# Query weights scaled later, shared down tiles moved behind the experts, and a norm begun one layer earlier, in a two-layer transformer kernel

## The chip, the cores and the metric

The kernel runs on one core of one Trainium2 chip. A core has five engines with queues of their own: TensorE (PE, with weight loads PEld beside it), VectorE (DVE), ScalarE (ACT), GpSimd (POOL) and SyncE (SP, which here issues most DMAs). Each engine takes its instructions in order and waits at the front of its queue for semaphores of the others. The metric is device microseconds (us) of one execution.

## The reference, cut to what matters

Two transformer layers work on the residual stream x of 4 sequences of 512 tokens, 256 wide. Each has an attention and an FFN half, each with a layer norm, a shift and scale, and a gate g from a conditioning vector c:

```python
h = layernorm(x) * (1 + ca) + sa;   x = x + ga * attention(h)
h = layernorm(x) * (1 + cb) + sb;   x = x + gb * ffn(h)
```

Layer 0's attention is linear (normalised q times a sum of normalised k times v). Its FFN is a mixture of 32 experts, 6 to a token:

```python
buf = zeros((E * C + 1, h)).at[slot].set(x[tok_idx])        # C = 48 places per expert
gu = einsum('ech,ehf->ecf', xb, w_gate_up); g, u = split(gu, 2)
yb = einsum('eci,eih->ech', silu(g) * u, w_down)
out = einsum('tk,tkh->th', topk_w, yflat[slot])
out = out + (silu(x @ ws_gate) * (x @ ws_up)) @ ws_down     # the shared expert
```

Layer 1's attention has 16 heads of 128 with a causal mask over T = 512 tokens of a sequence:

```python
logits = einsum('bthd,bThd->bhtT', q, k) * rsqrt(128);  out = softmax(logits + mask) @ v @ w_o
```

Its FFN is gated, with weights made from control points by a spline.

## The kernel before

**Order.** The order of PE is the order in which the code issues its matmuls; for the stretch around the change it is written out by hand (the block `tc.manual_schedule`, L953). The other engines' instructions are ordered by a scheduler by priority and readiness in its own model, except that `tc.issue_after(x)` puts what it encloses behind x on x's engine. An instruction without such a tie can be put far ahead of its place in the code. Buffers come from pools: a tile with `tag` and `bufs=n` is a ring of n, and a new tile waits until all work on the one n before it is done.

**Layer 0's end.** After the linear attention the 32 experts are done in 16 pairs, q = 0 to 15. `fetched(q)` (L793) gathers a pair's token rows, with their weights and target places, from a table in DRAM into a tile `xg` by an indirect DMA of POOL. `turned(q)` (L802) transposes them on PE, and DVE copies them to `xT`. `gate_up(q)` (L809) multiplies by the pair's weights; ACT makes silu, DVE the product `act`. `act_turned(q)` (L825) transposes that. `down(q)` (L832) makes `y`, which ACT weighs into `ysb` (a ring of four; pairs 12 to 15 have another four). Three things then leave `ysb`: an indirect DMA of POOL scatters it into the array `planes` in DRAM (pairs 0 to 11 only), a DMA of SP writes it to the table `ytab`, and, for pairs 12 to 15, `combined(q)` (L890) adds it on PE by a one-hot matrix. Expert weights `wg` and `wd` are in rings of eight, loaded on SP as slots come free.

The loop of L960 to L989 runs for each q, on PE: gate_up(q+1), act_turned(q), turned(q+2), one shared down in the first iterations, down(q-1), combined(q-2). `shared_down(i)` (L724) is the down product of the shared expert for token tile i of 16: three matmuls into a PSUM bank `pd`, and a copy to `ysum` by ACT. Before, tiles 0 to 3 stand ahead of the loop, 4 to 9 in its iterations 0 to 5, 10 and 11 around the last `combined`, and 12 to 15 at the end of the block. Only sequence 0 is combined here, to let layer 1 begin: `read_back` (L917) loads its sums from `planes` into `yr` once all scatters have landed, `gated` (L932) adds them to x on POOL and DVE, and `add_transposed` adds what pairs 12 to 15 gave. The other sequences are gathered from `ytab` later, under layer 1.

**Into layer 1.** `scale_q(n)` (L767) multiplies the query weights of head n by a constant, on ACT; the first three are issued at L1010, behind the block, with no tie. `norm(0)` (L1167, called at L1495) norms sequence 0: statistics on DVE, a power on POOL (L196, `last_pow`), the normed `xn` half on DVE and half on ACT, transposes on PE into `lt_a`, and `hT_a` from these by ACT and DVE. `hT` tiles are in a pool `hp1` (L1021). POOL then makes the first weight forms (`weight_forms`, L1183 to L1191, sums of blocks of weights, since products here use seven block products for eight).

**Layer 1's head loop** (L1519 to L1589) runs n = 0 to 64 over 4 x 16 heads. Among the work of a head are the next head's projections (`project`), scores, softmax and values of this and the one before, on POOL the weight forms of a later head, and one unit of the spline for the FFN weights in every second head. At units 1, 4 and 7, that is at heads 8, 14 and 20, four POOL subtractions `ffn_forms` (L1061) follow. Heads 11, 27 and 43 issue the next sequence's `norm`; heads around multiples of 16 issue gathers of `ytab`. Head 59 issues the norm of the FFN of sequence 0, `ffn_norm(0)` (L1082, L1586), untied.

## Time and profile before

| | |
|---|---|
| median of 3 executions | 1165.59 us (1163.98 to 1167.76) |
| profiled execution | 1165.69 us |
| its span | 1164.0 us, and 1.69 us around it |
| mean granted PE clock | 0.992 |
| busy, share of the span | PE 96%, PEld 71%, DVE 73%, POOL 53%, ACT 47% |
| DMA | 86.09 MB, mean 74 GB/s |

The experts lie between about 150 and 225 us, the passage into layer 1 up to about 245 us, the head loop up to the spline FFN at the end. A line of the timeline gives start, duration, engine, code line, operation, output and inputs, and in brackets how long the engine had been idle before it and what ended that. A line of the waits gives in total, how often and the longest wait of an engine at one place. PE can be granted half its clock after idle time, and the windows of the profile list what it was granted (1.00 is the full clock).

### The profile page before, as it was taken

How to read it: one execution, taken by the hardware profiler on the slowest of the kernel's cores; microseconds unless marked ns; L12 is line 12 of the kernel's file. 1: busy time of each engine (PE TensorE's matmuls, PEld its weight loads, DVE VectorE, ACT ScalarE, POOL GpSimd, SP SyncE). 2: the span in 40 equal slices, each digit the busy share in tenths (PEclk: the TensorE clock that was granted, in tenths of full speed). 3: DMA queues.
4: the chain of work that ended last, by engine and by line, in shares of the span. 5: the costliest groups of instructions: out<-in, count | busy, mean ns of one | idle time of the engine just before them, and what ended most of it. 6: DMA issues, size and time to landing. Idle time of an engine off the chain costs nothing.

```text
span 1164.0 us, 16910 instructions
## 1 busy us (share of the span) xinstructions
PE 1118.4 (96%) x5231; PEld 822.6 (71%) x5231; DVE 850.9 (73%) x2573; ACT 541.5 (47%) x1380; POOL 621.0 (53%) x944
## 2 busy tenths in 40 slices
PE   7888999989999999999999999999999999999998
PEld 2444364557777777777777777777787777888887
DVE  5687534567878887888887887988877777566765
ACT  3652223345555555555555465555555455333321
POOL 4363224248874857864656975444635655344331
PEclk9998999899999999999999999999999999999999
DMA  7921379734411322520321431012010000000001
GB/s 264 289 68 46 98 238 287 223 101 95 77 46 53 67 68 38 91 68 28 78 40 43 95 64 60 28 37 69 19 46 19 25 13 1 1 1 19 19 1 36
DMA packets 80485, 86.09 MB, mean 74 GB/s; under 512 B 12158, under 2 KB 64748, under 8 KB 80268
## 3 DMA queue, kind: packets, MB, share of 16 engines
q1 hardware_dynamic: 67868, 70.19, 19.3%
q0 software_dynamic: 11712, 13.25, 7.2%
q10 hardware_dynamic: 816, 1.58, 0.4%
q8 instruction: 42, 0.69, 0.2%
q14 instruction: 47, 0.39, 0.1%
HBM read 73.84 MB, written 11.55 MB: 73 GB/s over the span
## 4 chain that ended last, share of the span: by engine, by line
PE 72%; DVE 8%; POOL 4%; ACT 3%; issue 2%; DMA 2%; SPq 0%; ACTq 0%; POOLq 0%; DVEq 0%
PE s L1308 10%; PE o L1349 10%; PE po L1044 7%; PE P0p L1044 6%; PE fP L1044 6%; PE pt L1340 5%; PE P1p L1044 4%; PE P2p L1044 4%; PE acc L1044 3%; PE P0v L1044 3%; PE P2v L1044 2%; PE P1v L1044 2%; POOL ysum L281 1%; PE gu L814 1%; PE sg L713 1%
## 5 line engine op out<-in xcount | busy, mean ns | idle before, releaser
L1323 ACT ACTIVATE p<-s,nm 128x512 f32<-128x512 f32 (+3 forms) x256 | 135.4, 529 | 117.2 <-DVE nm L1320 114.7
L1308 PE MATMUL s<-qk,qk 128*128 128x512 f32 (+3 forms) x512 | 170.1, 434 | 1.1 <-DVE qk L1216 1.0
L1349 PE MATMUL o<-pT,v 128*128 128x512 f32 (+3 forms) x512 | 148.8, 433 | 0.3 <-DVE u3v L1228 0.3
L1349 PEld LDWEIGHTS o<-pT,v 128*128 128x128 f32 x512 | 96.8, 190 | 55.4 <-issue 30.6
L1342 ACT COPY pT<-pt 128x512 f32<-128x512 f32 (+1 forms) x192 | 98.5, 513 | 68.2 <-PE pt L1340 66.5
L1320 DVE TENSOR_REDUCE nm<-s 128x1 f32<-128x512 f32 (+3 forms) x256 | 124.0, 484 | 4.0
L281 POOL DMA_INDIRECT ysum<-ytab,code x72 | 113.6, 1578 | 20.4 <-issue 15.2
L1325 DVE TENSOR_SCALAR p<-p,den 128x512 f32<-128x512 f32 (+3 forms) x256 | 116.9, 457 | 3.4
L1340 PEld LDWEIGHTS pt<-ident,p 128*128 128x128 f32 x640 | 81.6, 141 | 34.5 <-issue 10.5
L1340 PE MATMUL pt<-ident,p 128*128 128x128 f32 x640 | 101.7, 273 | 0.3 <-DVE p L1325 0.3
L1318 DVE TENSOR_TENSOR s<-s,mask 128x128 f32<-128x128 f32 x256 | 73.5, 287 | 32.3 <-PE s L1308 32.3
L1183 POOL TENSOR_TENSOR w_p<-w_q,w_k 128x128 f32<-128x128 f32 x63 | 38.9, 617 | 84.3 <-ACT t1p L1222 51.9
L1308 PEld LDWEIGHTS s<-qk,qk 128*128 128x128 f32 x512 | 77.5, 191 | 5.5 <-issue 1.1
L1044 PE MATMUL P0p<-hT_a,w_q 128*128 128x256 f32 x252 | 75.0, 379 | 0.0
L1191 POOL TENSOR_TENSOR w_p<-w_k 128x128 f32<-128x128 f32 x63 | 29.9, 475 | 81.3 <-PE P2p L1044 81.3
L1044 PEld LDWEIGHTS P0p<-hT_a,w_q 128*128 128x128 f32 x252 | 47.5, 190 | 33.1 <-issue 29.9
L1324 DVE RECIPROCAL den<-den 128x1 f32<-128x1 f32 x256 | 40.4, 158 | 38.5 <-ACT p L1323 34.4
L1044 PE MATMUL P1p<-fT,w_p 128*128 128x256 f32 x252 | 65.0, 380 | 2.4 <-POOL w_p L1185 1.3
L1360 ACT ACTIVATE oH<-o,bia 128x512 f32<-128x512 f32 x64 | 44.0, 687 | 42.7 <-PE o L1349 41.5
L1216 DVE SCALAR_TENSOR_TENSOR qk<-P0p,bia,u3p 128x256 f32<-128x256 f32 x63 | 30.4, 482 | 37.4 <-ACT qk L1237 36.2
L1052 POOL TENSOR_TENSOR fI<-it 128x256 f32<-128x256 f32 x30 | 21.8, 728 | 67.0 <-DVE it L1641 67.0
L1044 PEld LDWEIGHTS P1p<-fT,w_p 128*128 128x128 f32 x252 | 47.6, 190 | 10.1 <-issue 2.2
(336 smaller groups left out, 2676.9 us busy)
## 6 DMA issues: line engine op xcount, KB each, us to landing
wg<-in_w_gate_up SPq DMA_DIRECT2D x16, 704.0 KB
w_q<-in_w_q SPq DMA_DIRECT2D x64, 128.0 KB
w_k<-in_w_k SPq DMA_DIRECT2D x64, 128.0 KB
w_v<-in_w_v SPq DMA_DIRECT2D x16, 512.0 KB
wd<-in_w_down SPq DMA_DIRECT2D x16, 352.0 KB
basis<-in_basis SPq DMA_DIRECT2D x8, 640.0 KB
planes<-zero SPq DMA_DIRECT2D x4, 768.0 KB
yr<-planes SPq DMA_DIRECT2D x4, 768.0 KB
```

The lines of the kernel that those rows point to most:

```text
L281: ga = nc.gpsimd.indirect_dma_start(out=ysum[b][:, i, :], out_offset=None, in_=ytab[:, :], in_offset=bass.IndirectOffsetOnAxis(ap=code[:, ...
L1044: nc.tensor.matmul(out, lhsT=lhsT, rhs=rhs, start=start, stop=stop, skip_group_check=shared)
L1308: nc.tensor.matmul(s[:, at[i] : c], lhsT=qk[n, 0][:, i * P : (i + 1) * P], rhs=qk[n, 1][:, : (i + 1) * P], start=True, stop=True,)
L1318: nc.vector.tensor_tensor(s[:, e - P : e], s[:, e - P : e], mask, ALU.add)
L1320: nc.vector.tensor_reduce(nm, s[:, e - w : e], AX.X, ALU.max, negate=True)
L1323: nc.scalar.activation(p, s[:, e - w : e], AF.Exp, bias=nm, accum_out=den)
L1324: nc.vector.reciprocal(den, den)
L1325: nc.vector.tensor_scalar_mul(p, p, den)
L1340: nc.tensor.transpose(pt[:, c : c + P], probs[n, i][:, j * P : (j + 1) * P], ident)
L1342: nc.scalar.copy(pT, pt[:, :w])
L1349: nc.tensor.matmul(o[:, j * P :], lhsT=vs[n // 4][:, j, hc : hc + HD], rhs=pTs[n, j], start=(j == 0), stop=(j == NTT - 1),)
L1360: nc.scalar.activation(oT, o, AF.Identity, bias=bia[:, 2, h : h + 1])
```

## The change

1. `scale_q(0)` to `scale_q(2)` are tied on ACT behind the copy of shared down tile 9, which now stands in the tail.
2. Three shared down tiles leave the loop (iterations 3 to 5). The tail has tiles 7 and 8 around the last `combined`, 9 to 14 behind it, and 15 behind the transposes of the norm. Tiles from 9 on alternate over two banks, `su0` and `su1`, by the new `NTAIL`.
3. The ring of `xg` has seven tiles for eight, and seven gathers are issued ahead for eight.
4. Layer 1's first norm is issued inside the block of layer 0: `xn` in a freed slot of the expert weights (class `Freed`), `lt_a` in the PSUM ring `gu`, `hT` in the pool `w4` with a ring of two; the pool `hp1` goes. ACT's half of `xn` is tied behind the copy of tile 13, and tile 15 stands behind the transposes on PE.
5. `ffn_forms` of units 0, 1 and 2 are issued at heads 8, 15 and 24, tied behind the last weight form.
6. `ffn_norm(0)` at head 59 is tied behind that head's eviction.

The number of instructions is the same on every engine.

```diff
+NTAIL = 7
@@ new_hT
-        return pool.tile([P, 2, T], F32, tag="hT", name=f"hT_{name}{b}")
+        return pool.tile([P, 2, T], F32, tag="hT", name=f"hT_{name}{b}", bufs=B if name[1] == "0" else 2)
@@ layer 0
+        class Freed:
+            def __init__(self, tag, pair):
+                self.tag, self.pair = tag, pair
+            def tile(self, shape, dtype, tag, name, bufs=None):
+                return freed(self.tag, self.pair, shape, name)
...
-            pd = psa.tile([P, D], F32, tag=f"su{i % 2 if i < NEXP or i >= NI - 4 else 0}", name=f"pd{i}", bufs=1)
+            pd = psa.tile([P, D], F32, tag=f"su{i % 2 if i < NEXP or i >= NI - NTAIL else 0}", name=f"pd{i}", bufs=1)
...
-                xg[q] = xp.tile([P, ROW], F32, tag="xg", name=f"xg{q}", bufs=8)
+                xg[q] = xp.tile([P, ROW], F32, tag="xg", name=f"xg{q}", bufs=7)
...
-                if q + 8 < NPAIR:
-                    fetched(q + 8)
-            for q in range(8):
+                if q + 7 < NPAIR:
+                    fetched(q + 7)
+            for q in range(7):
                 fetched(q)
...
-                    if q < NI - NEXP - 6:
+                    if q < NI - NEXP - NTAIL - 2:
                         shared_down(NEXP + q)
...
-                shared_down(NI - 6)
+                shared_down(NI - NTAIL - 2)
                 combined(NPAIR - 1)
-                shared_down(NI - 5)
+                shared_down(NI - NTAIL - 1)
...
-                for i in range(NI - 4, NI):
-                    last_down = shared_down(i)
+                for i in range(NI - NTAIL, NI - 1):
+                    pd_copy = shared_down(i)
+                    if i == NI - NTAIL:
+                        with tc.issue_after(pd_copy.ins):
+                            for n in range(3):
+                                scale_q(n)
+                    if i == NI - 3:
+                        before_norm = pd_copy
+                hTs1[0] = new_hT(w4, 0, "a1")
+                ln_transposed(
+                    Freed("wg", NPAIR - NLOAD + NTT), ps, "gu", 1, 0, SA, CA, hTs1[0], "a1", None, None, before_norm
+                )
+                with tc.issue_after(last_pow[0].ins):
+                    shared_down(NI - 1)
...
-        for n in range(3):
-            scale_q(n)
...
-    hp = ctx.enter_context(tc.tile_pool(name="hp1", bufs=2))
@@ head loop
-        norm(0)
+        EARLY_FORMS = (8, 15, 24)
...
-                if unit in (1, 4, 7):
-                    ffn_forms(unit // 3, early[:, unit // 3])
...
+            if n in EARLY_FORMS:
+                with tc.issue_after(last_form[0].ins):
+                    ffn_forms(EARLY_FORMS.index(n), early[:, EARLY_FORMS.index(n)])
...
-                ffn_norm(0)
+                ffn_norm(0, evicted[n])
```

## The prediction

> **What bounds the kernel.** I read the page's busy shares first, then TensorE's (PE's) waits, then the instructions around the long ones, then what the DMA engines did there. On the page:

> ```profile
> PE 1118.4 (96%) x5231; PEld 822.6 (71%) x5231; DVE 850.9 (73%) x2573; ACT 541.5 (47%) x1380; POOL 621.0 (53%) x944
> ```

> PE is busy for all but 46 us of the 1164.0 us span. The instruction counts of the changed kernel are the same on every engine, so it can only win PE's idle time, and matmul time spent at a lowered clock. PE's waits that the change touches:

> ```profile
> PE gu L814 <- DVE xT L807: 4.1, 1, 4.1
> PE lt_a L226 <- ACT xn_a L208: 3.0, 1, 3.0
> PE P2v L1044 <- DVE v L1215: 2.3, 3, 1.9
> PE P1p L1044 <- POOL w_p L1185: 1.3, 1, 1.3
> ```

> Columns: total us, times, longest. The first two stand between the experts and layer 1, the others inside the head loop. In the order of time the first looks like this (start, us, engine; in brackets the idle time and what ended it):

> ```profile
> 204.85 0.42 ACT L770 ACTIVATE w_q<-w_q 128x256 f32<-128x256 f32 x1 [5.22 <-DMA w_q<-in_w_q]
> 206.37 2.61 PE L814 MATMUL gu<-wg,xT 128*64 128x352 f32 x8 [4.07 <-DVE xT L807]
> 209.93 1.66 PE L837 MATMUL y<-wd,actT 88*64 88x256 f32 x8
> ```

> ACT stands still 5.22 us in a scaling that waits for its weights. Behind it on ACT are the activations of the expert pairs; DVE's xT stands behind their products, and PE runs dry. The stage table shows what follows (columns: PE, PEld, DVE, ACT, POOL busy, granted PE clock, DMA share, GB/s):

> ```profile
> 200.00:205.00 5.00, 2.30 (x18) 1.32 (x16) 0.42 (x1) 0.15 (x1) 0.00 (x0) 0.93 0.83 264
> 205.00:210.00 5.00, 3.63 (x14) 1.52 (x16) 2.91 (x20) 2.56 (x7) 1.57 (x3) 0.50 0.71 154
> 235.00:240.00 5.00, 2.04 (x9) 1.31 (x9) 2.73 (x8) 1.75 (x4) 4.12 (x7) 0.84 0.56 194
> 240.00:245.00 5.00, 4.99 (x13) 2.36 (x12) 2.33 (x6) 1.18 (x2) 1.44 (x3) 0.82 0.09 26
> ```

> After both idle times PE runs at half clock, and the DMA engines are still full at 205. The DMA rows of the same stretch say what comes next:

> ```profile
> 204.51 2.28 SPq L882 DMA_DIRECT2D ytab<-ysb  x3
> 212.86 1.02 POOL L867 DMA_INDIRECT planes<-ysb,didx  x1 [4.19 <-ACT ysb L851]
> 216.77 2.06 SPq L921 DMA_DIRECT2D yr<-planes  x4
> 223.14 0.96 DVE L937 TENSOR_TENSOR yr<-yr 128x768 f32<-128x768 f32 x1 [3.10 <-DMA yr<-planes]
> 238.40 2.13 PE L226 MATMUL lt_a<-ident,xn_a 128*128 128x128 f32 x8 [2.96 <-ACT xn_a L208]
> ```

> A chain runs from pair 11's output (ACT ysb, 211.64), the last that is scattered, through the scatter, the read-back, DVE's sums and the norm to lt_a: 238.40 - 211.64 = 26.76 us, with DVE busy without a gap over most of its last 15.26 (223.14 to 238.40). PE, with its shared downs done at 235.43, waits for it.

> **The change, part by part.** Times are before's span.

> 1. *Scaling tied late.* Gone are the 4.07 us of idle PE and the half clock behind it: gu13 2.61 for 1.38, act_t 0.66 for 0.46, xt 0.63 for 0.40, y11 1.66 for 1.08, together 2.2. So y11 ends 6.3 us earlier, at 205.3 for 211.59. The three scalings (0.42 each) now stand on ACT behind the copy of pd9. Their weights landed by 204.5. Behind them on ACT is the copy of pd10, which would otherwise wait 0.93 us for PE: 3 x 0.42 = 1.26 makes it 0.33 late, and the shared down that wants its bank is a whole one (1.34) later: 0.

> 2. *Three shared downs out of the loop* (4 to 9 become 4 to 6). An iteration with one took 4.12 us (y2 170.34, y3 174.46, y4 178.59), one without 2.88 (y5 181.42 to y6 184.30). A shared down is 5.36 / 4 = 1.34 us in the tail's row and 1.30 in the chain: 3 x 1.30 = 3.9. But where DVE also makes the codes an iteration without one took 3.55 (184.30 to 187.85), 0.67 more. Two of the three lie beside codes, which gives back up to 1.3. Ends 2.5 and 3.9; I take 3.0, nearer the low one because two of three have the codes row. y11 would end at 202.2.

> 3. *What is late next.* The ring of ysb has four buffers, so ysb11 waits until ysb7 is written to ytab. SP issues a DMA only when the one eight before it on SP has landed; ytab8 is eight behind ytab7 and issued at 204.51, with its data ready since 193, so ytab7 landed about then. The DMA share was 0.95 to 1.0 from 160 to 195 with the same bytes as after, so an earlier issue lands little earlier: between 203.0 and 205.0, I take 204.2. ysb11 thus moves from 211.64 to 204.2, -7.4, not -9.4. Behind it on ACT wait the activations of pair 13, and on PE y12, which needs the single y bank: PE idles about 1.2 there. From ysb11 the chain takes its 26.76, plus what the scatter loses in fuller queues: it landed 3.1 to 3.75 us after its start at pairs 10 and 11, and 6.2 to 7.3 earlier in the loop. Ends 0 and +2.5; I take +0.3, since it will start at 205.4, and pair 10's, which started at 206.72 before, was one of the quick ones. lt_a comes at about 231.3, **-7.1** (-9.2 to -4.6). PE now has two more shared downs ahead of lt_a (2 x 1.34) and reaches it at about 229.9: 1.4 us of idle. The nearest row is the 1.86 us at 769, which left the clock full, not the 2.96.

> [...]

> 4. *lt_a to the first attention product* (P0v, 244.71, 6.31 us after lt_a before, with 3.41 of it at half clock). Now: transposes 0.87, pd15 1.30, 0.57 until ACT has copied pd15 out of the bank that pj wants, products 3.5: 6.2, **-0.1**. If the clock halves again, +1.7. POOL's weight forms, 4.53 us, now start behind lt_a and not during it, and are first wanted 6.6 us after it: 0, with 2 to spare.

> 5. *Seven xg buffers for eight; SP's order.* A gather starts about 7.4 us ahead of PE's need of it where it was one iteration more; gathers landed in 6.2 to 7.3: 0, at most +0.5. wg12 is issued one load later, still some 8 us ahead of its landing's use; two win loads go behind wo, and nothing in the transition waits for either: 0.

> The norm itself is the same instructions on DVE, ACT and POOL as before, with its scalings on ACT tied behind the copy of pd13; what stands behind those on ACT (pd14, pd15) is wanted by nothing before pj. The load of basis moves behind pd15 on SP, and is read first by the spline of head 6: 0.

> 6. *Spline forms at heads 8, 15, 24 for 8, 14, 20.* Four POOL subtractions of 0.45 to 1.06 us (2.2 together at 495.3). At head 20 they stand behind four gathers (488.7 to 495.3) and ahead of w_p, which PE then waits 1.27 us for. At head 24 POOL has no gathers ahead of them and the 2.2 us lie in its idle time before a head's forms (3.7 us at 749.9): **-1.27** (-1.3 to 0). 14 to 15: 0.

> 7. *ffn_norm(0) tied behind head 59.* The scheduler had run its DVE, POOL and ACT steps at 751 to 768, where they met norm(3): DVE waited 0.91 for POOL's power and made xn in 1.40, v came late, and PE lost 1.86. norm(3) alone should cost what those at heads 11 and 27 did (0.59, 0.66): +0.6. The same norm at head 59 has no row; its bounds are 0.6 (those rows) and 1.9 (two norms together), I take 1.0, as it is one norm, but now PE's transposes stand right behind it. **-0.3** (-1.3 to +1.0).

> Sum: -7.1 - 0.1 - 1.3 - 0.3 = -8.8. The profiled execution was 1165.69 (span 1164.0 and 1.69 around it; the median is 0.1 less): **1156.9 us**.

> **Rivals.**
> - *B, the transfers don't hold pair 11.* The loop runs earlier from pair 3 on, so ytab7 may be in time. ysb11 at 202.25 puts lt_a at 229.0 to 229.3: -9.2, PE nearly without idle. Sum -10.8: 1154.9. For it: DMA share 0.82 from 195 to 200, so the queue was thinning. Against it: 13 us for ytab7's landing.
> - *C, the transfers hold harder.* ytab7 at 204.5, scatter 11 in 6.3 us as in the loaded stretch (+2.5), lt_a at 233.8, PE idle 3.6 and so the half clock (+1.7): -4.6 + 1.6 - 1.6 = -4.6, 1161.1. For it: the scatters and gathers of the loaded stretch, none of which took under 6 us. [...]
> [...]
> - *D, slower: the ring of seven becomes the loop's bound.* A gather can start only when ysb(q) has been read out, and its xt is four iterations on: an iteration is at least (3.6 + L) / 4, with 3.6 us for ysb, scatter and issue and L the landing. At 7.3 that is 2.73, under 2.88. Without a margin L = 12.3 would make 3.98, 1.1 more in each of eight gathers, 8.8 in all, and from there on the kernel is slower, with two such gathers more at 1168. For it: three shared downs of padding leave the loop. Against it: no gather above 7.3.

> **How the numbers follow.** A 0.55, B 0.12, E 0.03, C 0.20, D 0.10. No change is within 0.3% or 3.5 us, about what a measurement here can tell. A, B, E and 0.6 of C lie below 1162.1: faster 0.82; the rest of C and 0.03 of D the same: 0.11; slower 0.07. A alone spans 1155 to 1159.5 by the ends of its terms taken two at a time; the range reaches to B and C, 1153.5 to 1162.5, and leaves out D and the far ends, under 0.2.

> **What would show it.** Right: no idle of 4 us before gu13 and no half clock there; ysb11 near 204 behind a DMA; lt_a near 231 with 1 to 2 us of idle; no w_p wait near 499; the wait near 769 shrunk to about 0.6; a new one of about 1 near head 59. Wrong: gu or xt waiting for an xg gather in each iteration (D), a half clock at lt_a (C), or waits for POOL's forms just behind it.

## The result and the profile after

The changed kernel takes 1156.45 us (median of six, 1155.38 to 1158.41) where the kernel before took 1165.72 on the same chip: a ratio of 0.9919, 95% interval 0.9898 to 0.9939. Forecast was 1156.9. A second set of runs, with e9 below, gave 1157.79 (1156.17 to 1158.49) and 0.9944 (0.9926 to 0.9962). The profiled execution took 1155.95 us, its span 1154.2, 9.8 less than that of before.

The page's first line and, of PE's waits, what became of those shown of before and what is new (total us, times, longest):

```profile
PE 1115.8 (97%) x5231; PEld 820.8 (71%) x5231; DVE 849.8 (74%) x2573; ACT 541.0 (47%) x1380; POOL 620.1 (54%) x944
```

```profile
PE lt_a L227 <- DVE xn_a L213: 4.4, 4, 1.9
PE P2p L1065 <- POOL oWTrue L1396: 1.9, 3, 0.7
PE pj L1065 <- ACT ysum L746: 0.5, 1, 0.5
PE P2v L1065 <- DVE v L1235: 0.4, 2, 0.2
```

The waits of gu for xT (4.1) and of P1p for w_p (1.3) are gone, and P2v's is down from 1.9 to 0.2. lt_a's longest, 1.9, is now that of another sequence. Two small waits are new or larger: pj for the copy of tile 15, and P2p for POOL. In the loop gu now waits 1.3 in all, in two steps that item 2 below comes back to. The passage into layer 1 in the timeline (start, us, engine, idle time before and its end in brackets):

```profile
203.86 0.95 ACT L862 ACTIVATE ysb<-y,xg 64x256 f32<-64x256 f32 x2 [1.82 <-DMA ytab<-ysb]
205.12 1.08 PE L848 MATMUL y<-wd,actT 88*64 88x256 f32 x8
209.18 2.11 SPq L932 DMA_DIRECT2D yr<-planes  x4
215.52 1.46 DVE L948 TENSOR_TENSOR yr<-yr 128x768 f32<-128x768 f32 x1 [3.68 <-DMA yr<-planes]
230.05 1.47 PE L227 MATMUL lt_a<-ident,xn_a 128*128 128x128 f32 x8 [0.23 <-DVE xn_a L213]
233.29 1.99 PE L1065 MATMUL pj<-hT_a,w_q 128*128 128x512 f32 x4 [0.46 <-ACT ysum L746]
236.82 0.59 PE L1065 MATMUL P0v<-w_v,hT_a 128*128 128x256 f32 x2
```

```profile
200.00:205.00 5.00, 5.00 (x36) 2.67 (x36) 2.93 (x20) 2.36 (x6) 1.57 (x3) 1.00 0.84 252
205.00:210.00 5.00, 5.00 (x31) 2.37 (x30) 2.45 (x7) 2.35 (x6) 1.02 (x1) 1.00 0.61 162
235.00:240.00 5.00, 5.00 (x18) 3.17 (x17) 2.29 (x5) 1.75 (x4) 1.90 (x4) 1.00 0.36 128
```

ysb11 waits for a write to ytab, as forecast, at 203.86 for 211.64; lt_a stands at 230.05 for 238.40 and P0v at 236.82 for 244.71. In these three windows (columns as before: PE, PEld, DVE, ACT, POOL, clock, DMA share, GB/s) PE is busy throughout. Its clock record has no fall between 150 us and the last 3 us of the span.

**How the runs are compared.** The medians of one kernel move by up to 1.3 us between sets of executions (before 1164.52 to 1165.72, changed 1156.45 and 1157.79), and the profiles show one source: the first expert product, y0, starts between 158.72 and 163.91 us in the 14 profiled executions. These two extremes, e12 and e4, have the same code ahead of it. So beside the medians I give times counted from y0: to ysb11, to lt_a, and to the first head's output on ACT (oH), and how long PE was at half clock from 185 us on, without the last 3 us of the span, by the trace's clock records. In e5 and e10 two shared downs that stand ahead of y0 elsewhere are gone: from the first gate_up product to y0 they take 7.8 us, the twelve others 9.35. To compare these two rows with the others, take 1.6 off their three times from y0.

| kernel | median (range) | ratio to before (95%) | y0 at | ysb11 | lt_a | oH | half clock |
|---|---|---|---|---|---|---|---|
| before | 1165.72 (1163.57-1170.14) | 1 | 162.09 | 49.55 | 76.31 | 107.08 | 10.2 |
| changed | 1156.45 (1155.38-1158.41) | 0.9919 (0.9898-0.9939) | 162.51 | 41.35 | 67.54 | 98.78 | 0 |
| changed again, e9 | 1157.79 (1156.17-1158.49) | 0.9944 (0.9926-0.9962) | 162.31 | 42.33 | 68.65 | 99.88 | 0 |
| e1, scaling late alone | 1160.32 (1157.63-1162.21) | 0.9972 (0.9954-0.9990) | 160.88 | 42.58 | 70.26 | 101.53 | 3.4 |
| e13, parts 1, 5, 6 | 1158.51 (1156.37-1161.46) | 0.9950 (0.9936-0.9965) | 161.53 | 42.75 | 70.58 | 102.51 | 6.8 |
| e12, part 1 undone | 1161.41 (1156.77-1162.88) | 0.9972 (0.9958-0.9986) | 158.72 | 42.40 | 72.14 | 102.99 | 6.8 |
| e2, downs in loop | 1159.41 (1157.21-1159.88) | 0.9955 (0.9940-0.9970) | 161.34 | 43.71 | 71.01 | 104.06 | 6.8 |
| e5, ten downs late | 1160.66 (1157.45-1161.76) | 0.9965 (0.9951-0.9979) | 159.42 | 42.48 | 72.04 | 102.89 | 3.4 |
| e6, own buffers | 1156.70 (1155.83-1157.88) | 0.9934 (0.9917-0.9951) | 161.56 | 39.05 | 67.61 | 101.92 | 6.8 |
| e10, ten late, own buffers | 1156.78 (1154.60-1159.24) | 0.9931 (0.9909-0.9953) | 160.19 | 41.00 | 72.96 | 103.80 | 0 |
| e7, norm in layer 1 | 1157.87 (1155.57-1161.67) | 0.9944 (0.9922-0.9965) | 161.33 | 41.99 | 70.39 | 102.09 | 3.4 |
| e8, gather ring of six | 1161.31 (1158.14-1163.15) | 0.9968 (0.9956-0.9981) | 161.71 | 47.04 | 73.32 | 104.16 | 3.4 |
| e4, parts 5, 6 undone | 1157.22 (1153.66-1159.58) | 0.9931 (0.9910-0.9953) | 163.91 | 41.26 | 67.33 | 98.57 | 0 |
| e11, own buffers, all downs ahead of lt_a | 1153.90 (1153.15-1156.59) | 0.9918 (0.9899-0.9936) | 160.94 | 39.07 | 67.71 | 98.17 | 0 |

### The profile page after: what moved, and what is told of

It reads as the page before. It is cut to its first block, busy times and chain, and to the rows that moved or that the text cites. A ratio compares the mean times of both kernels' runs of the same rounds, so it can differ in the third digit from the quotient of the medians.

```text
span 1154.2 us, 16903 instructions
## 1 busy us (share of the span) xinstructions
PE 1115.8 (97%) x5231; PEld 820.8 (71%) x5231; DVE 849.8 (74%) x2573; ACT 541.0 (47%) x1380; POOL 620.1 (54%) x944
## 4 chain that ended last, share of the span: by engine, by line
PE 75%; DVE 8%; ACT 3%; issue 2%; POOL 2%; DMA 1%; SPq 0%; ACTq 0%; DVEq 0%; POOLq 0%
PE s L1328 11%; PE o L1369 10%; PE po L1065 8%; PE P0p L1065 7%; PE fP L1065 6%; PE pt L1360 5%; PE P1p L1065 4%; PE P2p L1065 4%; PE P0v L1065 3%; PE acc L1065 3%; PE P2v L1065 2%; PE P1v L1065 2%; PE gu L825 2%; PE y L848 1%; PE sg L724 1%
```

## The experiments

### What the scaling alone is worth (e1, e12, e13)

e1, on the kernel before:

```diff
                 for i in range(NI - 4, NI):
                     last_down = shared_down(i)
+                    if i == NI - 4:
+                        with tc.issue_after(last_down.ins):
+                            for n in range(3):
+                                scale_q(n)
...
-        for n in range(3):
-            scale_q(n)
```

> The kernel before with one edit: the three scalings tied on ACT behind the copy of shared down tile 12. Theory (half the stall is idle time, the rest is half clock, and the transfers do not yet bind): PE has no idle time before gu13, y11 ends at about 205.3 us for 211.59, ysb11 starts there (ytab7 lands by 204.5), lt_a comes at about 232.1 for 238.40 after some 3 us of idle PE, again at half clock. Gain 6.3, so about 1159.4 us. Rival 1 (only the idle time of 4.07 comes back, since the transfers hold ysb11 or the scatter is slow): a gain near 4, 1161.7. Rival 2 (the wait moves to another instruction that wants the same weights' transfers): no gain, 1165.7.

Measured: no wait before gu13, ysb11 6.97 earlier from y0 (49.55 to 42.58), of which 0.66 is one iteration of the loop that took 2.89 for 3.55. That leaves the forecast 6.3. lt_a comes 6.05 earlier from y0 (5.4 without that iteration), and PE stands before it for 3.83 us, with 3.4 us at half clock behind: as the theory has it. At the first head 4.9 of the 6.3 are left (107.08 to 101.53, less 0.66): from its issue to its second part at DVE the read-back took 7.26 us for 6.37, and lt_a to the first head 0.5 more than before. The median's gain, 0.28% or 3.3 us (1.2 to 5.4), is nearer rival 1's, and 6.3 lies outside its interval. In the profile it is 6.5 at the end of the span, 1.2 of it because y0 happened to come earlier. So the theory is borne out at pair 11, and what it forecast for the total is not.

e12, the changed kernel with the tie taken out again (the scalings stand in the code behind the block, untied):

```diff
-                    if i == NI - NTAIL:
-                        with tc.issue_after(pd_copy.ins):
-                            for n in range(3):
-                                scale_q(n)
...
+        for n in range(3):
+            scale_q(n)
```

> The changed kernel with part 1 alone undone: the three scalings stand behind the loop in the code with no tie, and fall between the activations of pairs 10 to 14 again. Theory: ACT waits behind ysb10 for w_q until about 204.5 us, PE idles 4 to 5 us before gu13 and runs at half clock behind it; the tiles taken out of the loop make the idle time only longer; y11 ends at 209 to 211 and lt_a comes 6 to 7.5 later than in the changed kernel: 1162.5 to 1164 us. Rival (most of the 9 us is the other parts'): 1159 or less.

Measured (timeline):

```profile
200.47 0.42 ACT L781 ACTIVATE w_q<-w_q 128x256 f32<-128x256 f32 x1 [4.08 <-DMA w_q<-in_w_q]
201.99 2.61 PE L825 MATMUL gu<-wg,xT 128*64 128x352 f32 x8 [4.25 <-DVE xT L818]
```

The stall is back with its half clock, and costs 3.5 to 4.6 at lt_a from y0 and 3.6 in the median against e9, measured beside it. That is less than the 6 to 7.5 expected at lt_a, and the median lies between the theory's 1162.5 and the rival's 1159: ysb11 is no later from y0 than in e9 (42.40 against 42.33), since there the ytab write holds it as long as the scaling does here. What is lost is PE's time; it now reaches lt_a last, with no idle time before it.

e13, e1 with parts 5 and 6 of the change added (`EARLY_FORMS`, `ffn_norm(0, evicted[n])`):

> The kernel before with parts 1, 5 and 6 alone: scalings tied late, spline forms at heads 8, 15, 24, FFN norm tied at head 59. No tile moved, ring of eight, norm in layer 1. Theory: the run e1 and 1.7 us less (1.0 and 0.7): 1157.5 to 1159 us, so that the moved tiles, the ring and the early norm together are worth 1 to 2.5 of the 9 us. Rival (the tiles and the norm carry a third of the gain or more): 1160 or more.

1158.51, as the theory has it. Against e9 on the same chip the moved tiles, the smaller ring and the early norm are worth 0.7 us (the intervals of the two ratios overlap), and at the first head, from y0, 2.6 to 3.7, of which 1.9 to 3.0 are there already when lt_a starts. So most of the gain is parts 1, 5 and 6: by the medians on that chip 6.0 of 6.7 us, and at the first head, which parts 5 and 6 don't reach, 4.6 of 7.2 to 8.3.

### What moving the downs does (e2, e5, e10, e6)

e2, the changed kernel with `if q < NI - NEXP - 6`, tiles 10 and 11 around `combined`, and a tail from `NI - 4`:

> The changed kernel with tiles 4 to 9 of the shared down back in loop iterations 0 to 5 and four in the tail, all else as changed. Theory (moving them pays only until ytab7 is written): y11 ends about 2 us later, at 205.4, and ysb11 starts there with no wait for a DMA, 1.5 us later than the 203.86 of the changed kernel; lt_a comes 1.5 later, at 231.6, and PE, with three tiles fewer ahead of it, idles 3 to 4 us there, which brings the half clock back (+1.7). 1158.0 to 1159.7 us. Rival (shared downs are padding wherever they stand): the changed kernel's 1156.5.

Measured:

```profile
205.05 0.95 ACT L862 ACTIVATE ysb<-y,xg 64x256 f32<-64x256 f32 x2 [2.46 <-DMA ytab<-ysb]
232.35 2.04 PE L227 MATMUL lt_a<-ident,xn_a 128*128 128x128 f32 x8 [5.37 <-DVE xn_a L213]
230.00:235.00 5.00, 2.65 (x10) 2.27 (x11) 1.91 (x8) 2.12 (x4) 1.44 (x2) 0.53 0.03 9
```

PE stands 5.37 us before lt_a, 6.8 us at half clock follow, and the median is 1.6 to 3.0 above the changed kernel's. But ysb11 did wait for ytab, which the theory had excluded: it was not y11 (202.79, against 202.24) that moved ysb11. In this run the tiles' worth is on the other side of the chain: in the tail they keep PE at work while the read-back runs.

e5, the changed kernel with `NTAIL = 10`:

> The changed kernel with NTAIL 10: tiles 4, 5 and 6 too leave the loop for the tail. Theory (pair 11 is held by the writing of ytab7 to about 203.5, whatever PE does): y11 ends near 200, ysb11 waits about 3.5 us for a DMA, PE idles 3 to 4 us before y12 and runs at half clock behind it (1.7 to 2.2), lt_a is no longer waited for but reached late, with the three tiles more ahead of it: at 233.5 to 235.2 for 230.05. 1160 to 1161.7 us, slower than the changed kernel. Rival 1 (tiles out of the loop keep paying, 1.3 us each): 1153 to 1154. Rival 2 (neutral padding): 1156.5.

Measured (ACT, four outputs in a row, then PE):

```profile
186.90 0.95 ACT L862 ACTIVATE ysb<-y,xg 64x256 f32<-64x256 f32 x2 [2.12 <-DMA ytab<-ysb]
192.25 0.95 ACT L862 ACTIVATE ysb<-y,xg 64x256 f32<-64x256 f32 x2 [4.06 <-DMA ytab<-ysb]
197.51 0.95 ACT L862 ACTIVATE ysb<-y,xg 64x256 f32<-64x256 f32 x2 [3.49 <-DMA ytab<-ysb]
201.90 0.95 ACT L862 ACTIVATE ysb<-y,xg 64x256 f32<-64x256 f32 x2 [3.09 <-DMA ytab<-ysb]
198.52 1.44 PE L848 MATMUL y<-wd,actT 88*64 88x256 f32 x8 [1.70 <-ACT ysb L862]
```

1160.66, 3 to 4 slower than the changed kernel: the theory's total. The wait is spread over pairs 8 to 11, not all at pair 11: these outputs start 0.85, 2.86, 3.17 and 1.94 us after their products end. Counted from the first gate_up product, ysb11 comes at 50.24 us for 50.70 (51.68 in e9), 0.5 to 1.4 earlier, though 3.9 us of work left the loop. The last pairs then go at the pace of the writes to ytab.

e6, the changed kernel with buffers of their own for pairs 9 to 11:

```diff
-                ysb = xp.tile(
-                    [P, D], F32, tag=("ysb", "ysd")[direct], name=f"ysb{q}", bufs=4
-                )
+                if 9 <= q < 12:
+                    ysb = freed(*(("wd", 8), ("wd", 9), ("wg", 13))[q - 9], [P, D], f"ysb{q}")
+                else:
+                    ysb = xp.tile(
+                        [P, D], F32, tag=("ysb", "ysd")[direct], name=f"ysb{q}", bufs=4
+                    )
```

> The changed kernel with the outputs of pairs 9, 10 and 11 in freed expert weight slots, so that their ysb waits for no earlier write to ytab. Theory (the ring of four holds pair 11): no ysb after pair 8 waits for a DMA; ysb11 starts 0.1 us behind y11, where the changed kernel's waited 0.5 us and those of the runs with loop downs and with the old forms 1.2 and 2.2; y12 no longer waits for it. 0.3 to 1.5 us faster than the changed kernel, 1155.0 to 1156.2 us, with PE the limit at lt_a. Rival (the scatter and the read-back are late whatever ysb11 does, because the same transfers are in their way): ysb11 earlier, lt_a unmoved, 1156.5.

Measured:

```profile
200.61 0.95 ACT L865 ACTIVATE ysb<-y,xg 64x256 f32<-64x256 f32 x2 [1.33 <-PE y L848]
201.84 1.02 POOL L881 DMA_INDIRECT planes<-ysb,didx  x1 [1.75 <-DMA w_q<-in_w_q]
207.52 2.09 SPq L935 DMA_DIRECT2D yr<-planes  x4
214.73 0.96 DVE L951 TENSOR_TENSOR yr<-yr 128x768 f32<-128x768 f32 x1 [5.65 <-DMA yr<-planes]
229.17 1.48 PE L227 MATMUL lt_a<-ident,xn_a 128*128 128x128 f32 x8 [2.11 <-DVE xn_a L213]
230.00:235.00 5.00, 4.54 (x13) 2.87 (x14) 3.21 (x5) 1.24 (x3) 4.13 (x6) 0.57 0.14 32
```

The rival won. ysb11 comes 2.3 us earlier from y0 and waits for PE alone, but the read-back is issued 5.68 us after the scatter starts for 4.09 in the changed kernel, and its second part reaches DVE 7.21 us after that for 6.34: 2.5 us given back to the transfers, lt_a unmoved (67.61 from y0 for 67.54; 68.65 in e9). From 205 to 210 us the DMA share was 0.83, for 0.61 in the changed kernel. PE, no longer held at y12, stands 2.11 us before lt_a, and that brings the half clock.

e10, e6 with `NTAIL = 10`:

> Ten late downs as in the run e5, and the own output buffers of the run e6. Theory (what made ten late downs slow is the ring of ysb, not the tiles' place): ysb9 to ysb11 wait for no DMA, PE does not stand before y11, and the time comes back from 1160.7 to between the run e6 and 1.5 us above it, since gu14 and gu15 now come near the landings of their weights (198 and 202.6 us in the kernel before): 1156 to 1158. Rival (a loop without padding runs into its loads and gathers anyway): PE idles by as much at gu or xt, 1160 or more.

1156.78, in the theory's range and 3.9 below e5, so by the medians the ring of ysb was what made ten late downs slow. The profiles don't show it: e10's, the slowest of its four executions, reaches the first head later from y0 than e5's (103.80 for 102.89), though ysb9 to ysb11 wait for no DMA in it. ysb7 and ysb8, still in the ring, came 2.91 and 3.85 us after their products and held PE for 2.39 before y8. gu waited 1.62 us for its weights, as the rival named, and the read-back was issued 9.04 us after the scatter's start, for 4.52 in e5. So the cause of e5's loss is likely, and not shown.

### The early norm (e7), and tile 15 ahead of the transposes (e11)

e7, the changed kernel with `norm(0)` called in layer 1, its ACT half tied behind the copy of the last of seven tail downs:

> The changed kernel with the norm of sequence 0 called in layer 1 again, and all seven tail downs ahead of its transposes. Theory (with PE busy up to lt_a the early norm is worth next to nothing): lt_a one shared down (1.3) later, but pj behind it at once and not behind the copy of pd15, POOL's forms beside the norm's DVE steps again (0.5 to 0.7 there): pj within 0.5 us of the changed kernel's 233.29, total 1156.3 to 1157.3 us. Rival (the early norm carries the passage): lt_a 2 to 3 us late with idle PE, 1159.

Measured:

```profile
231.72 0.41 PE L227 MATMUL lt_a<-ident,xn_a 128*128 128x128 f32 x2 [1.28 <-ACT xn_a L209]
232.31 0.87 PE L227 MATMUL lt_a<-ident,xn_a 128*128 128x128 f32 x6 [0.17 <-DVE xn_a L213]
233.62 3.67 PE L1056 MATMUL pj<-hT_a,w_q 128*128 128x512 f32 x4 [0.43 <-ACT hT_a L229]
```

pj starts at 233.62, 0.33 after the changed kernel's (from y0 1.5 after it, and 0.4 after e9's), but at half clock, 3.67 us for 1.99. At the first head it is 2.2 to 3.3 later from y0; the median, 1157.87, is the changed kernel's second one, 1.4 above its first and 0.6 above the theory's range. By the total the early norm is worth between nothing and 1.4 us, nearer the theory than the rival; in the changed kernel's two profiles the clock stayed up, and in this one it did not.

e11, e6 with tile 15 moved ahead of the norm's transposes:

```diff
-                for i in range(NI - NTAIL, NI - 1):
+                for i in range(NI - NTAIL, NI):
...
-                with tc.issue_after(last_pow[0].ins):
-                    shared_down(NI - 1)
```

> The run e6 (own output buffers) with tile 15 too ahead of the norm's transposes. In e6 PE stood 2.11 us before lt_a and ran 6.8 us at half clock. Theory (the clock falls when PE stands for more than some 1.8 us of one fixed window of 3.41 us): PE reaches lt_a 1.3 later and idles 0.8, and 0.9 more for hT, which keeps the clock in most executions: pj at about 231.2 for 233.29 in the changed kernel, P0v at 234.7 for 236.82, 2 us faster than the changed kernel, 1154.5 us. Rival (two short stands with transposes between count as one, as in the run e7, where 1.28, 0.17 and 0.43 us halved the clock): pj takes 3.7 for 2.0, P0v at 236.5, and 1156.2 us, the changed kernel's time.

Measured:

```profile
228.65 1.48 PE L227 MATMUL lt_a<-ident,xn_a 128*128 128x128 f32 x8 [0.89 <-DVE xn_a L213]
231.13 1.96 PE L1066 MATMUL pj<-hT_a,w_q 128*128 128x512 f32 x4 [1.00 <-DVE hT_a L233]
```

The two stands are 0.89 and 1.00 us, the clock stays up, and pj starts at 231.13 where 231.2 was expected. 1.6 of its 2.2 us ahead of the changed kernel's pj are y0's, though; from y0 it comes 0.6 earlier, and 1.7 earlier than e9's, and the first head likewise. 1153.90 us is the lowest median. Beside e9's 1157.79 on the same chip the ratios to before are 0.9918 (0.9899 to 0.9936) and 0.9944 (0.9926 to 0.9962); the changed kernel's first set, on another chip, had 0.9919. So e11 was faster than the set measured beside it (five of its six executions are below that set's fastest, and the ratios, whose intervals overlap, are 3.0 us apart), and by its ratio no different from the first set: the 2 us of the theory are not shown in full. The own buffers alone don't do it: e6 frees PE and wastes it before lt_a. Tile 15's move without them was not run.

### The gather ring (e8)

The changed kernel with `bufs=6`, `fetched(q + 6)` and `range(6)`:

> The changed kernel with six xg buffers and six gathers ahead. Rival D's formula, iteration at least (3.6 + L) / 3 with gathers landing in L = 6.2 to 7.3 us, gives 3.3 to 3.6 us for 2.88: PE waits for xt from pair 6 on, 0.4 to 0.75 in each of some nine iterations, y11 3.6 to 6.5 later, about 0.5 of it hidden by the wait for ytab7: 3 to 6 slower, 1159.5 to 1162.5 us. If gathers land in less than 5 us, or the loop's pace is set by something else: 1156.5.

```profile
177.40 0.48 PE L816 MATMUL xt<-ident,xg 128*128 128x128 f32 x2 [3.01 <-DMA xg<-table,idx]
189.22 0.48 PE L816 MATMUL xt<-ident,xg 128*128 128x128 f32 x2 [2.98 <-DMA xg<-table,idx]
```

3.5 to 4.9 slower, as rival D's formula has it for six, with the time in two waits of 3 us and not in nine small ones: the gathers that they wait for had started at 169.51 and 181.54, so they took 7.8 and 7.5 us to land. Of the three sizes run, seven is the smallest that costs nothing at xt: in the changed kernel no xt waits for a gather.

### The steps in layer 1 (e4, e9)

e4, the changed kernel with `EARLY_FORMS = (8, 14, 20)` and `ffn_norm(0)` untied:

> The changed kernel with the spline forms at heads 8, 14, 20 and the first FFN norm at head 59 untied, both as before. Theory: PE waits 1.0 to 1.3 us for POOL's w_p near head 20 again, and the FFN norm meets the attention norm of sequence 3 at heads 41 to 43 again (1.3), while the 0.6 us near head 58 goes: 1.7 us slower, 1158.2. The place of the first layer's experts stays to 0.1 us. Rival (the steps in layer 1 seen between the two profiles are the spread of single executions): 1156.5, with steps elsewhere.

e9, the changed kernel once more:

> The changed kernel once more, for a second profiled execution. Theory: the steps in layer 1 return to 0.1 us against the profile of before (1.0 won near head 20, 1.3 near heads 42 and 43, 0.6 lost near head 57); the start of pair 0, the landing of ytab7 and so ysb11 (203.9 in the first profile) move by up to 2 us from execution to execution. Median 1156 to 1157 us. If instead the steps in layer 1 differ by as much, they are spread, not effects.

The start of each head's output on ACT, less that of before, changes in steps (us; minus is won):

| stretch of heads | changed | again, e9 | e13 | e11 | e4 | e1 |
|---|---|---|---|---|---|---|
| 20 to 21 | -0.97 | -0.97 | -1.49 | -0.97 | -0.05 | +0.01 |
| 26 to 28 | -0.41 | -0.41 | -0.41 | -0.39 | 0.00 | -0.41 |
| 41 to 43 | -1.32 | -1.23 | -1.33 | -1.33 | 0.00 | +0.10 |
| 57 to 58 | +0.56 | +0.55 | +0.55 | +0.55 | 0.00 | 0.00 |

Rows one, three and four come with parts 5 and 6 and go with them: they are effects, 1.0 (1.5 in e13 and three other runs) and 0.7 to 0.8 net. The second row stands in e1, which has neither, and not in e4: it changes between executions. The medians don't show the 1.7 us that e4 was expected to lose: its ratio is 0.9931, and the mean of the changed kernel's two, 0.9919 and 0.9944, is 0.9932. Such a step is under what these medians resolve; the profiles resolve it. e9's median, 1157.79, lies 0.8 above the range expected of it.

## Why the prediction was right

1156.9 was forecast and 1156.45 measured. The mechanism was right: the stall goes, the write to ytab holds pair 11 next, and the chain behind it sets lt_a. That the total came within 0.5 us is partly luck. The terms did not all come as they were put, their errors went both ways, and the second set of the same kernel came 0.9 above the forecast.

1. *Scaling*: -6.3 at y11. e1 has 6.3 at ysb11, with 4.9 left at the first head. Right in size and place.
2. *Three downs out of the loop*: -3.0 with ends 2.5 and 3.9. From y0 to y11 e1, with all in the loop, takes 41.44, the changed kernel 39.73 and 38.89 (e9), and e4, e6, e7 and e11 37.9: 1.7, 2.6 and 3.5. The row of 3.55 that I read as the price of the codes is not that: in e1, with the same codes, it takes 2.89, and in e6 the three iterations in which codes fall take 3.01, 2.89 and 2.89 for 2.88. It is a step of about 0.7 to 1.1 us that comes in some executions at some pair (before at pair 7, changed at pairs 4 and 6, e9 at pair 5). So the term was mis-sized by a wrong cause, and it mattered little, because of the next.
3. *What is late next*: ysb11 at 204.2, held by ytab7, and not at y11. 203.86, with the wait in the trace, and 204.64 in e9; y12 at 205.15 by the forecast, 205.12 measured. The place of ysb11 decided the forecast. The wait itself was 0.54 us behind the end of y11 in the changed kernel's profile, where y11 came late by item 2's steps, and 2.35 in e9. (The DMA share that I gave as 0.95 to 1.0 from 160 to 195 was 0.81 and 0.93 in two of those windows.) From ysb11 to lt_a 26.19 and 26.32 (e9) for the 27.1 put: the scatter cost 0.2 extra (4.09 to the read-back's issue; before 3.91), and DVE's last steps were shorter, which I had left out. Before, then changed:

```profile
236.96 0.69 DVE L203 SCALAR_TENSOR_TENSOR nmr_a<-ag_a,rs_a 128x4 f32<-128x4 f32 x1 [1.16 <-POOL rs_a L196]
237.57 1.36 DVE L212 TENSOR_SCALAR xn_a<-x,ag_a,rs_a 128x256 f32<-128x256 f32 x2
```

```profile
229.42 0.16 DVE L204 SCALAR_TENSOR_TENSOR nmr_a<-ag_a,rs_a 128x4 f32<-128x4 f32 x1 [1.16 <-POOL rs_a L197]
229.50 0.73 DVE L213 TENSOR_SCALAR xn_a<-x,ag_a,rs_a 128x256 f32<-128x256 f32 x2
```

Before, POOL made weight forms beside these; now it starts them behind lt_a. I priced that move at nothing, by asking only who waits for the forms and not whom they slow. It won 1.2 us of DVE time, and the chain is 0.6 shorter. The runs bear this out: the first of these rows takes 0.69 us in the four profiles in which `norm(0)` is called in layer 1 and the forms run beside it (before, e1, e13, e7), and 0.16 in the changed kernel, e2, e5, e6 and e8 to e12. The two rows take 0.69 and 1.36 us beside POOL's forms and 0.16 and 0.73 without; what of POOL's work slows DVE there was not shown.

lt_a came 8.35 earlier (7.44 in e9) for the 7.1 put, inside its bounds; PE stood 0.23 (0.49 in e9) for 1.4.
4. *lt_a to P0v*: 6.2 put, 6.77 measured. The transposes took 1.47, not 0.87, since they now follow xn as it is made; the 0.46 wait for pd15's copy is there (0.57 put). No half clock, as taken.
5. *Ring of seven, SP's order*: nothing, as put; e8 shows the edge one buffer away.
6. *Spline forms*: -1.27 put, -0.97 measured, twice; the step is -1.5 in four other runs.
7. *FFN norm*: -0.3 put, -0.76 and -0.68 measured. Near head 43 the wait left is 0.65 for the 0.6 put. At the new place 0.56 is lost, not 1.0; the trace names no wait of PE there, so where it goes stays open.

The sum at the end of the span was -9.8 where -8.8 was put: -8.35 at lt_a, +0.46 from there to P0v, -0.97 and -0.76 for the forms and the norm, the -0.41 near head 26 that changes between executions, and some 0.3 lost behind the last head.

The rivals: B (no hold) did not come, and e6 shows that it would not have paid: the transfers take the time back, as C had it in part. C's half clock came in the runs where PE stood longer at lt_a (e1, e2, e6, e7, e13), not in the changed kernel. D needed a ring one smaller. E, which has 0.03 in the chances and counts there as faster, took the scatter to be so quick that PE, and not the chain, sets lt_a. No run shows a scatter of that speed: the quickest, e8's, let the read-back go 2.94 us after its start, for 3.91 before, 4.09 in the changed kernel and 5.68 in e6.

Open: what moves y0 by 5 us between executions (all of it arises in the first 101 us; from there to the first shared down taken out the 14 profiles keep step; no run tests what it is), and the step of 0.7 to 1.1 us in single iterations of the loop.

## What to carry to other kernels

A short wait on a shared in-order engine costs what stands behind it on all engines, and here half as much again by the clock (4.07 us of idle PE before gu13, and 2.2 more at half clock); look for instructions without an order of their own that wait for a late load. When a stall goes, look for the buffer ring and the transfers behind it before counting the whole of it as won: pair 11 was held by the write of pair 7's output to DRAM, and freeing it only moved the wait to the scatter and the read-back. Work that nothing waits for (the shared downs) was worth most as cover at the place where the chain ends last. Its exact place there counts too: e11 differs from e6 in tile 15 alone and is 1.9 us faster by the ratios, though their intervals overlap, and 3.75 us earlier at the first head from y0.

## What the runs showed of the hardware

In e7 a fall in a busy stretch cost 1.7 us of PE time (pj 3.67 for 1.99 us), which is as much as several of the edits studied here; such falls may be part of why one kernel's executions differ.
